# Rankings of the first sequence split by head, with their ends in PSUM and on ScalarE

## The chip, the cores and the metric

The kernel runs on one core of a Trainium2 chip. The engines are TensorE (PE in the profile: matmuls; PEld: loads of its stationary operand), VectorE (DVE), ScalarE (ACT), GpSimd (POOL) and SyncE (SP, which here only issues DMAs). The metric is the device time of one execution in microseconds (us), the median of several runs. All data are fp32.

## The reference

```python
x = x + rnn(layernorm(x))            # x: 2 sequences x 2048 tokens x 256
x = x + ffn(layernorm(x))

# ffn: attention with 8 heads of 64; 5 experts for the values and 5 for the output, 2 chosen
gl_v = (x @ Ws).reshape(b, t, h, e)              # value gates
wv   = topk_mask(gl_v, 2) * sigmoid(gl_v)
xv   = einsum('btd,edk->btek', x, Wv)            # expert values, the same for all heads
v    = einsum('bthe,btek->bhtk', wv, xv)
attn = softmax(q * scale @ k.T) @ v
mask_o = topk_mask((x @ Wd).reshape(b, t, h, e), 2)   # output gates: only a mask
out  = einsum('bthe,bthk,ekd->btd', mask_o, attn, Wo)
```

So every token has, for each of 8 heads, five value logits and five output logits. The two largest of each five are kept. Value gates are the mask times a sigmoid; output gates are the bare mask.

## The kernel before

The recurrent part runs first (to about 124 us) and leaves the first sequence's normalised tokens, transposed, in `xT_of[0]`. The rest is one long loop over **steps** W. The attention has 16 heads (8 of each sequence); each head's queries are cut into 4 blocks of 512, which makes 64 units, and a unit's keys are cut into 8 tiles. A step computes four score tiles (`scores`, L589, into a pool of three PSUM buffers), VectorE moves each to SBUF with a running minimum (`stage`, L605), and two steps later, when a unit's minimum is known (`find_low`, L616 and L618), ScalarE takes the exponentials (L621), GpSimd adds tiles up for the denominator (`add_up` and `join`, L628 to L639), and TensorE multiplies the tiles with the values (`products`, L648). So a head takes 8 steps and the second sequence begins at step 64. Engines work through their own queues in the order in which the program issues instructions.

What else belongs to a step is put in five tables by hand: `head` (issued first), `mid`, `one` (after the four scores and stages), `vec` (after the products of the step) and `two` (last). Order in one step: `head`; exponentials of the tiles two steps old; four scores with their stages; `one`; products; in odd steps `take`, ScalarE's copy of a unit's result (L659); `vec`; `two`.

The change concerns the gates:

- `experts(b, j)` multiplies two chunks of 128 tokens with the value experts and both gate matrices at once (L530). ScalarE copies the expert values to `xw` (L537) and the 80 logits of each token to the tile `gl` (L544); `xw` goes to DRAM.
- `choose` ranks the logits of 8 chunks for all heads at once. The rank array starts at 4, 3, 2, 1, 0 (ScalarE copies `base`, L183). For each difference d = 1 to 4, `pair(d)` compares expert e with expert e+d (L192, into the PSUM tile "m", of which there is one buffer), adds the result to the later expert's rank and takes it from the earlier one's (L193, L194). A rank below 1.5 is chosen. `settle` makes the sigmoid from an exponential taken at the start (L181, L182, then L199, L200), multiplies it with the mask (L201), and makes the output mask (L202). `find_low` and `gate` use the same PSUM tile "m".
- `mix` and `mix_sum` build a head's values from the gates and `xw`: for head 0 GpSimd multiplies (L571), for later heads VectorE does (L574), reading a copy of the gates that ScalarE puts in PSUM (`gate`, L558); VectorE sums (L579). A later head's expert values come back from DRAM (`fetch`, L552).
- `weigh` and `masked` (L703 to L723) apply the output gates to a unit's result, in odd steps, in the last entries of `vec`.

Before the loop come keys part 0, queries part 0 and experts 0 and 1. Step 0 then holds keys part 1, experts 2 and 3 (all in `one`), the ranking "a0" of chunks 0 to 7 and two products of gates (`vec`). Step 1 holds experts 4 to 7, queries part 1 and the ranking "a1" of chunks 8 to 15. The second sequence is ranked in ten pieces, "b0" in steps 35, 37, 39, 41, 43 and "b1" in steps 45, 47, 49, 51, 53 (`at(vec, 35 + 10 * k + 2 * j, f)`).

## Time and profile before

| what | value |
|---|---|
| three runs | 1423.73, 1426.01 (median), 1427.76 us |
| the profiled execution | 1424.15 us |
| its span, first to last instruction | 1422.3 us |
| TensorE busy | 1339.2 us (94%) |
| VectorE busy | 1135.1 us (80%) |
| GpSimd busy | 1009.3 us (71%) |
| ScalarE busy | 703.0 us (49%) |
| first product (L648) of steps 2 to 7 | 190.33, 197.53, 207.38, 215.52, 224.95, 233.09 us |
| two steps, where nothing else is going on (as 250 to 340 us) | 17.57 us |
| GpSimd adds L628, L632 | 2613, 2379 ns |
| head fetch, issue to landing | 3.9 us |

A line of the timeline or of a group has start, duration, engine, line, operation, what it writes and reads, and its shape (partitions x elements). In brackets stands how long the engine had been idle before it and what released it. A line of the waits has who waited for whom, the total in us, how many times and the longest. L numbers are lines of the kernel before, unless said otherwise.

### The profile page before, as it was taken

Reading aid. Unit: us, or ns where it says so; the run is one execution under the profiler, and the core shown is the slowest. Engines: PE = TensorE matmul, PEld = TensorE weight load, DVE = VectorE, ACT = ScalarE, POOL = GpSimd, SP = SyncE. Lnnn points to the kernel's source line nnn. Section 1 sums busy time; section 2 is a strip of 40 time slices with the busy share of each in tenths; the row PEclk is TensorE's granted clock in tenths of the full one; section 3 lists DMA queues with packets and bytes.
Section 4 is the critical chain, followed back from the end, with each engine's and each line's share of the span. In section 5 each row is a group of like instructions: output and inputs, shape, how many; then the busy total and the mean of one; then the engine's idle time right before and its main releaser. Section 6 shows DMA issues by size and latency. Waiting matters only on the chain.

```text
span 1422.3 us, 36420 instructions
## 1 busy us (share of the span) xinstructions
PE 1339.2 (94%) x15450; PEld 634.3 (45%) x15450; DVE 1135.1 (80%) x2104; ACT 703.0 (49%) x911; POOL 1009.3 (71%) x590
## 2 busy tenths in 40 slices
PE   6999689999899999989999999999999999999986
PEld 5896234444344444333344454444444444444444
DVE  6666589999877787889888787888888888888753
ACT  3434255555356556444555445555555555555451
POOL 1101168888687777778798776888888888888960
PEclk9999889999899999999999999999999999999999
DMA  6012136666666666566577555566766676767643
GB/s 193 1 67 79 63 97 155 161 146 142 130 145 146 141 132 143 120 136 132 122 162 172 123 145 142 152 134 135 150 135 149 137 151 136 150 137 151 137 106 100
DMA packets 66315, 187.00 MB, mean 131 GB/s; under 512 B 8928, under 2 KB 26464, under 8 KB 66144
## 3 DMA queue, kind: packets, MB, share of 16 engines
q0 software_dynamic: 25056, 97.53, 37.1%
q1 hardware_dynamic: 39456, 86.46, 19.2%
q8 instruction: 123, 2.02, 0.6%
q10 hardware_dynamic: 1632, 0.61, 0.2%
q14 instruction: 48, 0.39, 0.1%
HBM read 59.79 MB, written 50.33 MB: 77 GB/s over the span
## 4 chain that ended last, share of the span: by engine, by line
PE 58%; issue 15%; DVE 11%; POOL 4%; ACT 1%; DMA 1%; DVEq 0%; POOLq 0%; ACTq 0%
PE o L648 28%; PE s L589 12%; DVE p L605 7%; PE pq L505 4%; PE pk L488 4%; PE pz L825 3%; PE pv L530 3%; PE pc L667 2%; PE pc L680 1%; POOL es L632 1%; POOL es L628 1%; POOL es L638 1%; PE pl L616 1%; PE py L809 1%; DMA es<-p 1%
## 5 line engine op out<-in xcount | busy, mean ns | idle before, releaser
L605 DVE TENSOR_SCALAR_CACHE_REDUCE p<-s 128x1024 f32<-128x1024 f32 x512 | 596.4, 1221 | 116.2 <-PE s L589 114.0
L621 ACT ACTIVATE p<-p,low 128x1024 f32<-128x1024 f32 x512 | 546.1, 1140 | 54.9 <-DVE low L618 54.5
L589 PE MATMUL s<-q,k 64*32 64x512 f32 x4096 | 482.5, 603 | 13.7 <-DVE p L605 10.4
L589 PE MATMUL s<-qs,k 64*32 64x512 f32 x4096 | 482.5, 603 | 11.1 <-DVE p L605 5.8
L648 PE MATMUL o<-p,v 128*64 128x256 f32 x4096 | 472.4, 383 | 0.0
L628 POOL TENSOR_TENSOR es<-p,p 128x1024 f32<-128x1024 f32 x126 | 329.2, 2613 | 164.5 <-ACT p L621 164.5
L648 PEld LDWEIGHTS o<-p,v 128*64 128x64 f32 x4096 | 282.8, 137 | 194.6 <-ACT p L621 47.8
L632 POOL TENSOR_TENSOR es<-es,p 128x1024 f32<-128x1024 f32 x126 | 299.8, 2379 | 9.9
L659 ACT COPY os<-o 128x256 f32<-128x256 f32 x64 | 23.8, 372 | 394.7 <-PE o L648 394.7
L589 PEld LDWEIGHTS s<-qs,k 64*32 64x32 f32 x4096 | 120.7, 107 | 147.7 <-issue 75.9
L589 PEld LDWEIGHTS s<-q,k 64*32 64x32 f32 x4096 | 120.6, 107 | 147.0 <-issue 67.6
L638 POOL TENSOR_TENSOR es<-es,es 128x1024 f32<-128x1024 f32 x63 | 151.4, 2403 | 4.9 <-DMA es<-p 4.8
L634 POOL DMA_DIRECT2D es<-p x126 | 110.0, 873 | 19.1 <-POOL es L632 15.2
L574 DVE TENSOR_TENSOR pr<-xq,pw 128x1280 f32<-128x1280 f32 x60 | 89.3, 1488 | 31.1 <-ACT pw L558 31.1
L723 DVE TENSOR_TENSOR pro<-pc,mr 128x1280 f32<-128x1280 f32 (+1 forms) x65 | 95.6, 1471 | 2.2
L579 DVE TENSOR_REDUCE v<-pr 128x256 f32<-128x1280 f32 x64 | 94.9, 1485 | 2.1
L639 POOL TENSOR_TENSOR es<-es 128x512 f32<-128x512 f32 x63 | 85.5, 1358 | 4.9
L488 PE MATMUL pk<-xT,wk 128*32 128x512 f32 x512 | 62.2, 604 | 2.0 <-ACT xT L408 0.5
L505 PE MATMUL pq<-xT,wq 128*32 128x512 f32 x512 | 62.1, 603 | 1.4
L739 POOL DMA_DIRECT2D yd<-pro x48 | 56.7, 1181 | 0.8 <-DVE p L605 0.8
L571 POOL TENSOR_TENSOR pr<-xw,gates 128x1280 f32<-128x1280 f32 x4 | 11.0, 2775 | 52.2 <-DVE gates L201 52.2
L530 PE MATMUL pv<-wvg,xT 128*128 128x400 f32 x128 | 47.6, 522 | 0.0
(141 smaller groups left out, 977.2 us busy)
## 6 DMA issues: line engine op xcount, KB each, us to landing
es<-p POOLq DMA_DIRECT2D x126, 512.0 KB, 4.8
xq<-xvd SPq DMA_DIRECT2D x60, 640.0 KB, 3.9
yd<-pro POOLq DMA_DIRECT2D x48, 640.0 KB, 8.0
qs<-q SPq DMA_DIRECT2D x64, 128.0 KB, 2.3
xvd<-xw SPq DMA_DIRECT2D x8, 640.0 KB, 3.2
yd<-pro SPq DMA_DIRECT2D x8, 640.0 KB, 4.1
y<-yd SPq DMA_DIRECT2D x8, 640.0 KB, 4.8
x<-in_x SPq DMA_DIRECT2D x16, 256.0 KB, 5.1
```

What stands on the lines that cost most here:

```text
L488: nc.tensor.matmul(pk[g * R : (g + 1) * R], lhsT=wk[:, kc, d0 : d0 + R], rhs=xc[:, kc, c0 // 2 : (c0 + HC) // 2, o, :], start=kc == 0, sto ...
L505: nc.tensor.matmul(pq[g * R : (g + 1) * R, :], lhsT=wq[:, kc, d0 : d0 + R], rhs=xT_of[b][:, kc, n * QB : (n + 1) * QB], start=kc == 0, sto ...
L579: nc.vector.tensor_reduce(v_of[i][:, 4 * part : 4 * part + 4, :], pr, AX.X, ALU.add)
L589: nc.tensor.matmul(ss[g * R : (g + 1) * R, o, :], lhsT=k_of[i][half, c, g * R : (g + 1) * R], rhs=q_of[i, n][o][half, :], start=True, stop ...
L605: nc.vector.tensor_scalar(p, ss, 1.0, None, ALU.mult, ALU.min, accum_out=part_of[u][:, c : c + 1])
L621: nc.scalar.activation(ring[t], ring[t], AF.Exp, scale=-1.0, bias=low_of[t // HC])
L628: nc.gpsimd.tensor_tensor(e, ring[t], ring[t - 1], ALU.add)
L632: nc.gpsimd.tensor_tensor(e, e, ring[t], ALU.add)
L634: nc.gpsimd.dma_start(out=es_of[u, half], in_=ring[t], accum_op=ALU.add)
L638: nc.gpsimd.tensor_tensor(e, e, es_of.pop((u, 1)), ALU.add)
L648: nc.tensor.matmul(o_of[u][g * DH : (g + 1) * DH, :], lhsT=v_of[i][:, 2 * c + o, :], rhs=ring[t][:, o, g * QH : (g + 1) * QH], start=c == ...
L723: nc.vector.tensor_tensor(o_of["p", u][:, s0:s1], po[:, s0:s1].unsqueeze(2).to_broadcast([P, w, E, 2, DH]), o_of["m", u][:, s0:s1].unsquee ...
```

## The change

`choose` now takes a range of chunks and a range of heads. The first sequence is ranked in four parts: a0 (chunks 0 to 7, head 0) in step 0; a2 (chunks 0 to 7, heads 1 to 7), and after it a1 (chunks 8 to 15, head 0), in step 1; a3 (chunks 8 to 15, heads 1 to 7) in pieces in step 2 (d = 1), step 3 (d = 2 and 3) and step 4 (d = 4 and the end). The second sequence keeps its ten pieces. All logits of a sequence lie in one tile, each comparison is issued once for the value and once for the output logits, the rank array starts one lower (so that 0.5 divides), and the sigmoid is made wholly at the end, in a PSUM tile "m"; ScalarE makes the output mask with two Relu operations. keys part 1 is issued after experts 2 and 3. Head 1's mixes move from steps 3, 4, 6, 8 to 4, 5, 6, 8, and their fetches with them.

```diff
-        nc.gpsimd.memset(base[:, e : e + 1], float(E - 1 - e))
-
-    def choose(pool, scratch, b, c0, nm):
+        nc.gpsimd.memset(base[:, e : e + 1], float(E - 2 - e))
+
+    def choose(pool, scratch, b, c0, c1, h0, h1, nm):
...
+        def part(t, kind):
+            v = t.rearrange("p c (t h e) -> p c t h e", t=2, e=E)[:, c0:c1, :, h0:h1, :]
+            return v if kind is None else v[:, :, kind]
 
         def begin():
-            got[0] = pool.tile([P, G, E], F32, tag="rank", bufs=1, name=f"rank{nm}")
-            gv = gt[:, :, 0:HE]
-            nc.vector.tensor_scalar(gv, gl_of[b, c0 // HN][:, :, 0:HE], -87.0, None, ALU.max)
-            nc.scalar.activation(gv, gv, AF.Exp, scale=-1.0)
-            nc.scalar.copy(got[0], base.unsqueeze(1).to_broadcast([P, G, E]))
+            got[0] = pool.tile([P, n, 2, m, E], F32, tag="rank", bufs=1, name=f"rank{nm}")
+            for k in range(2):
+                nc.scalar.copy(
+                    got[0][:, :, k],
+                    base.unsqueeze(1).unsqueeze(1).to_broadcast([P, n, m, E]),
+                )
 
         def pair(d):
...
-            above = scratch([P, G, w], f"ge{nm}_{d}")
-            nc.vector.tensor_tensor(above, g[:, :, 0:w], g[:, :, d:], ALU.is_ge)
-            nc.vector.tensor_tensor(rank[:, :, d:], rank[:, :, d:], above, ALU.add)
-            nc.vector.tensor_tensor(rank[:, :, 0:w], rank[:, :, 0:w], above, ALU.subtract)
+            above = scratch([P, n, 2, m, w], f"ge{nm}_{d}")
+            for k in range(2):
+                nc.vector.tensor_tensor(
+                    above[:, :, k], g[:, :, k, :, 0:w], g[:, :, k, :, d:], ALU.is_ge
+                )
...
+            nc.vector.tensor_tensor(up, up, above, ALU.add)
+            nc.vector.tensor_tensor(down, down, above, ALU.subtract)
 
         def settle():
-            rank = got[0].rearrange("p (c g) e -> p c (g e)", c=8)
-            gv = gt[:, :, 0:HE]
-            nc.vector.tensor_scalar(gv, gv, 1.0, None, ALU.add)
-            nc.vector.reciprocal(gv, gv)
-            nc.vector.scalar_tensor_tensor(gv, rank[:, :, 0:HE], 1.5, gv, ALU.is_lt, ALU.mult)
-            nc.vector.tensor_scalar(gt[:, :, HE:], rank[:, :, HE:], 1.5, None, ALU.is_lt)
+            rank = got[0]
+            gv, gm = part(gates_of[b], 0), part(gates_of[b], 1)
+            sg = scratch([P, n, m, E], f"sg{nm}")
+            nc.vector.tensor_scalar(sg, part(gl_of[b], 0), -87.0, None, ALU.max)
+            nc.scalar.activation(sg, sg, AF.Exp, scale=-1.0)
+            nc.scalar.activation(gm, rank[:, :, 1], AF.Relu)
+            nc.scalar.activation(gm, gm, AF.Relu, scale=-1.0, bias=unit)
+            nc.vector.tensor_scalar(sg, sg, 1.0, None, ALU.add)
+            nc.vector.reciprocal(sg, sg)
+            nc.vector.scalar_tensor_tensor(gv, rank[:, :, 0], 0.5, sg, ALU.is_lt, ALU.mult)
...
-    for k in range(2):
+    for part in range(4):
+        k = part // 2
+        if part % 2 == 0:
+            if k:
+                for p in range(2):
+                    at(vec, 1, mix_sum, 0, p)
+                for f in choose(ap, misc, 0, 0, HN, 1, H, "a2"):
+                    at(vec, 1, f)
+            for f in choose(ap, misc, 0, k * HN, (k + 1) * HN, 0, 1, f"a{k}"):
+                at(vec, k, f)
+        at(vec, k, mix, 0, part)
...
-        else:
-            at(one, 0, keys, 0, 1)
...
-                W = max(3, W0 - 6 + 2 * part)
-                at(two if W == 3 else head, W - 1, fetch, i, part)
+                W = (4, 5, 6, 8)[part] if i == 1 else W0 - 6 + 2 * part
+                at(two if i == 1 and part in (1, 2) else head, W - 1, fetch, i, part)
...
+    at(one, 0, keys, 0, 1)
     at(one, 1, queries, 0, 1)
+    for j, f in enumerate(choose(ap, misc, 0, HN, NCH, 1, H, "a3")):
+        at(vec, 2 + (j + 1) // 2, f)
...
-        for j, f in enumerate(choose(ap, misc, 1, k * HN, f"b{k}")):
+        for j, f in enumerate(choose(ap, misc, 1, k * HN, (k + 1) * HN, 0, H, f"b{k}")):
             at(vec, 35 + 10 * k + 2 * j, f)
```

## The prediction, made before the changed kernel was run

> **What bounds the kernel now.** The page first: the 1422.3 us span has TensorE busy for 94%, and the chain that ended last gives it 58% and VectorE 11%. That is an average, so next came the timeline and waits of the stretches that hold rankings: steps 0 to 7 (134 to 236 us, step W beginning with its first score) and the second sequence's steps 35 to 53 (500 to 710 us). Waits from 134 to 204 us:
>
> ```profile
> POOL pr L571 <- DVE gates L201: 52.2, 2, 29.7
> ...
> DVE gates L181 <- ACT gl L544: 15.4, 2, 9.2
> ...
> PE s L589 <- DVE p L605: 9.7, 1, 9.7
> ...
> PE pl L616 <- DVE ranka L194: 7.3, 1, 7.3
> ```
>
> TensorE stands still twice for rankings: 9.7 us in step 1 (scores find no free buffer, since VectorE ranks until 156.99) and 7.3 us before step 2, where find_low's transpose needs the one-buffer PSUM tile that the ranking's comparisons use. The second ranking starts late, on ScalarE and VectorE:
>
> ```profile
> 174.76 0.60 ACT L515 ACTIVATE q<-pq 128x512 f32<-128x512 f32 x1 [1.00 <-PE pq L505]
> 175.25 0.46 ACT L182 ACTIVATE gates<-gates 128x320 f32<-128x320 f32 x1
> 175.61 0.71 ACT L183 COPY ranka<-base 128x640 f32<-128x640 f32 x1
> ```
>
> ```profile
> 173.79 0.33 DVE L181 TENSOR_SCALAR gates<-gl 128x320 f32<-128x320 f32 x1 [9.16 <-ACT gl L544]
> 174.04 0.69 DVE L192 TENSOR_TENSOR gea<-gl 128x512 f32<-128x512 f32 x1
> 176.36 0.69 DVE L193 TENSOR_TENSOR ranka<-ranka,gea 128x512 f32<-128x512 f32 x1 [1.63 <-ACT ranka L183]
> ...
> 182.24 2.15 DVE L200 RECIPROCAL gates<-gates 128x320 f32<-128x320 f32 x1
> ...
> 184.84 0.32 DVE L202 TENSOR_SCALAR gates<-ranka 128x320 f32<-128x320 f32 x1
> 185.07 0.28 DVE L618 TENSOR_REDUCE low<-pl 128x1 f32<-128x128 f32 x1
> ```
>
> The rank array's first fill stands in ScalarE's queue behind all expert copies and the q copy. From there to step 7's first stage, busy times of PE, PE's loads, VectorE (39.20 of 44.71 us: little slack), ScalarE, GpSimd:
>
> ```profile
> 185.07:229.78 44.71, 44.22 (x548) 18.19 (x540) 39.20 (x65) 27.99 (x32) 38.88 (x19) 0.97 0.50 124
> ```
>
> The second sequence:
>
> ```profile
> 652.13 1.51 DVE L192 TENSOR_TENSOR geb<-gl 128x256 f32<-128x256 f32 x1
> 653.67 0.46 DVE L193 TENSOR_TENSOR rankb<-rankb,geb 128x256 f32<-128x256 f32 x1
> ...
> 689.69 1.37 DVE L199 TENSOR_SCALAR gates<-gates 128x320 f32<-128x320 f32 x1
> 691.09 2.15 DVE L200 RECIPROCAL gates<-gates 128x320 f32<-128x320 f32 x1
> ```
>
> ```profile
> 650.29 3.02 POOL L628 TENSOR_TENSOR es<-p,p 128x1024 f32<-128x1024 f32 x1
> 653.38 2.50 POOL L632 TENSOR_TENSOR es<-es,p 128x1024 f32<-128x1024 f32 x1
> ```
>
> ```profile
> 691.88 0.37 ACT L659 COPY os<-o 128x256 f32<-128x256 f32 x1 [6.86 <-PE o L648]
> ```
>
> A comparison worth 0.45 us (151.50) takes 1.51: it ends just after GpSimd's L628. GpSimd's next add, 2.37 alone, is stretched to 2.50. The two exclude each other and take turns.
>
> **The change, part by part.** Prices are rows of the trace of before: VectorE pair operations 0.69, 0.57, 0.45, 0.39 us for 512, 384, 256, 128 elements and 0.17 for 20; reciprocal 2.15 for 320 and 0.19 for 4; ScalarE 0.47 for 320 and 0.17 for 20. Between them I interpolate; dependent ones add 0.03.
>
> Step 0. keys(0,1) moves behind experts 2 and 3 (5.64 us): 138.35 to 144.0, logits copied at 144.95 instead of 146.77. But the k copy now stands ahead of the rank fill: keys end 145.9, copy 146.45, two fills of 40 by 146.9 (first rank operation 148.28 before). Step 1's scores, which read these keys, wait 0.7 us more; hidden, VectorE ranks until later. Ranking a0 (8 chunks, head 0): 14 operations of 0.2 to 0.25 = 3.0, then maximum 0.2, exponential on ScalarE 0.26, add 0.2, reciprocal 0.45, select 0.2: end 151.3 (156.99 before). GpSimd's two products start there and stay hidden.
>
> Step 1. Four stages of 1.145 and "one" to 156.1, two mix sums to 159.1. TensorE: fourth score at 152.6 to 154.4, experts 4 to 7 (twice step 0's 5.64, or 12.6 as after the 9.7 us wait) to about 166.4, queries 1.9 to 168.3, q copy, then the fills of ranking a2 (7 heads, two of 280, 0.84): its first rank operation at about 169.7. So a2 cannot use the gap under the experts: only its first comparisons run there. a2: ranks 2 x 0.65, then pairs 1.8, 1.45, 1.1 = 5.65; end 0.46 + 0.49 + 0.46 + 1.95 + 0.47 = 3.8; done 179.2. a1 (chunks 8 to 15, head 0): fills wait for a2's rank buffer, 0.45 + 3.0 + 1.35 = 4.8; done T = 184.0 (182.9 to 186 with the experts' bounds). The old ranking ended 185.07, so 1.1 is gained; but find_low's transpose, at 182.03 before, now waits for a1's end, its sigmoid lying in the same PSUM tile. First product of step 2: T + 8.3 as before from the transpose: 192.3 against 190.33, **+2.0**.
>
> Steps 2 to 6. a3, another 10.9 us of VectorE work (pairs 2.1, 1.8, 1.6, 1.2, end 4.2), enters where 5.5 of 44.7 were idle; GpSimd's queue keeps its order. Step 2: pair 1 fits ahead of step 3's scores, 0. Step 3: head 1's mix (3.0) goes to step 4, pairs 2 and 3 (3.4) come, and the transpose waits for the comparison tile: +2.0 at step 4's product. Step 4: mix 3.0, pair 4 and the end. Its exponential stands in ScalarE's queue ahead of step 5's four exponentials (4.27): they move from 28 to 36 us after T. The pair meets GpSimd's join (stall 2.0). VectorE begins step 5's stages at T + 38 instead of T + 32, the fourth score waits for a buffer: +5.8. Step 5 now has mix, statistics, weigh and masked (6.1) behind its stages; masked frees a score buffer late: +2.7. From step 7 the pace is TensorE's again (17.57 per two steps), and nothing is won back. SyncE's queue: head 1's fetches go out one at a time, parts 0, 1, 2 a little later; each still follows the mix that frees its buffer by 3.9 to landing and has 7 us or more: 0; without that lead a mix would wait, 3.9 at most. The mask and weight copies of head 1 on ScalarE move with the mixes. First products of steps 2, 4, 5, 6, 7: 192, 211, 225, 237, 245 against 190, 207, 216, 225, 233. Sum **+12.4** (8 to 16).
>
> Second sequence. Each comparison becomes two, the second waiting for the first: 0.15 each, and the first loses an operation (-0.33). The price is the port: after the first half GpSimd's waiting add goes, the second half waits 2.4. Rows where two adds follow on (528.14, 548.67, 634.07, 653.38, 672.24): five, at steps 37, 39, 47, 49, 51. Steps 37 and 39 have 1.4 and 2.2 idle, leaving 1.4 and 0.8; the others 2.6 each: **+10.0** (bounds 0.6, if both halves pass together, and 13). The ends, steps 43 and 53: the exponential now stands behind the copy of o, which waits for the step's products. At 53: maximum 689.6 to 690.1, exponential 692.25 to 692.7, add 0.48, reciprocal 2.17, select 0.49: 695.9 against 694.0; at 43 595.7 against 593.4. Both lie on the chain (before: L199 to L723, then scores): **+4.1** (2 to 6). In PSUM the 320 element operations have no row of before: 0.32 to 0.49, taken at 0.48.
>
> No cost: one logits tile instead of two, the other constants, the masks on ScalarE (read first by weigh, a step or more later; two of 0.47 instead of VectorE's 0.32; without that cover the 0.6 more would fall on six endings, under 4 us). Relu has no row: at worst it reloads the function table, 1.28 once (5.55), two loads in six endings, 15 us; at best 0. I take 0: Identity, Tanh, Exp and copies ran here on a single load. The Trainium skill, "ScalarE: Activation LUTs", section "Table sets: the hidden batching unit", says that cheap functions such as relu lie in every set: by it 0 too. [...] "SBUF — State Buffer", in the consequences of its port table, says that a VectorE instruction with two SBUF inputs and a GpSimd one block each other whole and that issue order decides. It would credit the endings moved to PSUM with the stalls of L199 (0.5 and 1.05) and L181 (2.1), some 3.6 us; my sum has these, and finds more put back by halving.
>
> Sum: 12.4 + 10.0 + 4.1 = 26.5 on the profiled execution's 1424.15 (span 1422.3, 1.85 around it): **1450.6**; that execution is 1.9 under the median of three.
>
> **Rivals.**
> A, the forecast: 1450, chance 0.55.
> B, both halves of a comparison pass GpSimd together: the second sequence's 10.0 falls to 0.6, step 4's stall by 1.4: 1424.15 + 11 + 4.7 = 1440. For: consecutive operations leave gaps of 0.03. Against: L632's stretches show GpSimd already waiting. 0.2.
> C, a2 runs under the experts: VectorE idles from 159 to 169.7; T falls by 10.5, 1440 (1430 with B). Against: the queue order that L183 shows. 0.13.
> D, not slower: TensorE sets the pace and VectorE's added work is slack. For: 94% and 58%. Then steps 3 to 7 keep their 42.7, the second sequence its time: +2, 1426. It decides if steps 3 to 6 hold under 8.8 us of VectorE work; step 6 held 8.2 of 8.8 before, and 689 to 697 is VectorE's alone. 0.08. A further 0.04: faster, by some gain not seen.
>
> **How the numbers follow.** A alone spans 1443 to 1457; with B and C the range is 1435 to 1458. Under 0.3% (4.3 us) a measurement here tells nothing. Faster 0.04; same 0.06 (most of D); slower 0.90.
>
> **What would show it.** Right: a2's first rank operation near 169.7, behind two ScalarE fills; step 7's first product some 12 us later than before; second halves of comparisons near 2.7 us at steps 47, 49, 51; an idle of about 2.6 before the add of one (L215 of the changed kernel) at steps 43 and 53, released by ScalarE. Wrong: a2 under the experts, step 5's exponentials on time, or two-step periods unchanged near 650 us.

## The result and the profile after

The changed kernel takes **1447.4 us** (median of four runs, 1445.6 to 1449.23) against 1424.87 (four runs) before: a ratio of **1.0156**, 95% interval 1.0133 to 1.0179. It is slower by 22.5 us. The forecast was 1450. Executions of one kernel lie up to 0.5% apart, the longer ones with a lower mean granted clock of TensorE (the kernel before: 1422.46 us at 0.986, 1429.18 us at 0.980). The profiled execution took 1448.38 us with a span of 1446.6, that is 24.3 more than the span before.

The page of the changed kernel, busy time by engine and then the chain that ended last:

```profile
PE 1342.9 (93%) x15450; PEld 636.5 (44%) x15450; DVE 1154.6 (80%) x2156; ACT 709.0 (49%) x933; POOL 1009.7 (70%) x590
...
PE 64%; DVE 15%; issue 14%; POOL 3%; DMA 2%; ACT 2%; SPq 0%; DVEq 0%; ACTq 0%; POOLq 0%
```

TensorE, ScalarE and GpSimd do what they did before, within 6 us. VectorE works 19.5 us more (1154.6 against 1135.1), and its share of the chain went from 11% to 15% (TensorE's from 58% to 64%). That already says in which queue to look, but not where.

To find the places, take one event that both kernels have in every odd step, ScalarE's copy of a unit's result `o`, and subtract its start in the profile before from its start in another profile. This **delay** rises where time is lost and stays level where nothing happens. What VectorE does at the end of an odd step shows at the copy of the next odd step. In us:

| profile | first stage | 3 | 5 | 7 | 9 | 35 | 43 | 45 | 53 | 55 | 127 |
|---|---|---|---|---|---|---|---|---|---|---|---|
| kernel before, a second profile | 0.7 | 0.8 | 0.9 | 0.8 | 0.8 | 0.9 | 0.9 | 0.9 | 0.9 | 0.9 | 0.7 |
| changed kernel | 1.4 | 2.5 | 11.1 | 12.4 | 12.8 | 12.1 | 13.2 | 14.7 | 21.8 | 23.3 | 24.3 |

So the 24.3 us consist of 1.4 before the first stage, where no code was changed; 11.4 up to step 9, the first sequence's rankings; 1.1 for the comparisons of steps 35 to 41 and 7.1 for those of steps 45 to 51; 1.5 and 1.6 for the endings at steps 43 and 53; and about 0.3 for the rest. The second row of the table shows what such a difference is worth: two profiles of the same program are 0.7 to 0.9 apart. These are sums by place and not yet by cause: in steps 4 and 5 a part is TensorE's granted clock ("Steps 3 to 7" below).

Steps 0 and 1, waits from 134 to 204 us of the changed kernel (who waited for whom, the total, how many times, the longest):

```profile
PE pl L630 <- DVE gates L217: 15.8, 1, 15.8
ACT sga L212 <- DVE sga L211: 12.9, 3, 6.3
DVE ranka L204 <- ACT ranka L184: 11.3, 2, 9.9
PE s L603 <- DVE p L619: 2.9, 1, 2.9
```

The wait of the scores for VectorE fell from 9.7 to 2.9 us: head 0 alone is ranked sooner. But two waits have come in its place. VectorE waits 9.9 us for the fill of a2's rank array, and the transpose of `find_low` (L630) waits 15.8 us instead of 7.3 for a ranking, now for its last instruction. ScalarE's timeline there, and VectorE's:

```profile
169.44 0.60 ACT L530 ACTIVATE q<-pq 128x512 f32<-128x512 f32 x1 [1.00 <-PE pq L520]
169.93 0.74 ACT L184 COPY ranka<-base 128x280 f32<-128x280 f32 x2
```

```profile
159.94 0.82 DVE L197 TENSOR_TENSOR gea<-gl 128x224 f32<-128x224 f32 x2
170.71 0.62 DVE L204 TENSOR_TENSOR ranka<-ranka,gea 128x448 f32<-128x448 f32 x1 [9.94 <-ACT ranka L184]
...
185.73 0.29 DVE L632 TENSOR_REDUCE low<-pl 128x1 f32<-128x128 f32 x1 [0.56 <-PE pl L630]
...
222.15 1.22 DVE L619 TENSOR_SCALAR_CACHE_REDUCE p<-s 128x1024 f32<-128x1024 f32 x1
```

The two fills are at the end of ScalarE's queue, behind the expert copies and the q copy, just as the fill was before; a2's comparisons are ready at 160.8 and the first rank operation starts at 170.71. Step 5's first stage (L619) starts at 222.15.

The second sequence, step 47 and the ending at step 53, on VectorE, then GpSimd at step 47 and ScalarE at step 53:

```profile
647.47 3.86 DVE L197 TENSOR_TENSOR geb<-gl 128x192 f32<-128x192 f32 x2
...
714.38 0.50 DVE L215 TENSOR_SCALAR sgb<-sgb 128x320 f32<-128x320 f32 x1 [2.44 <-ACT sgb L212]
```

```profile
645.63 3.04 POOL L642 TENSOR_TENSOR es<-p,p 128x1024 f32<-128x1024 f32 x1
648.75 2.35 POOL L646 TENSOR_TENSOR es<-es,p 128x1024 f32<-128x1024 f32 x1
```

```profile
713.65 0.37 ACT L673 COPY os<-o 128x256 f32<-128x256 f32 x1 [6.87 <-PE o L662]
713.92 0.43 ACT L212 ACTIVATE sgb<-sgb 128x320 f32<-128x320 f32 x1
```

The two halves of one comparison take 3.86 us together. They begin while GpSimd's L642 is running and end at 651.33, just after L646 ends at 651.10: the second half has waited for a whole further add. In step 53 the exponential (L212) starts behind the copy of `o`, which waits for the products, and VectorE is idle 2.44 us.

### The profile page after: what moved, and what is told of

Its sections match the earlier page's. It is cut to its first block, busy times and chain, and to the rows that moved or that the text cites. A ratio compares the mean times of both kernels' runs of the same rounds, so it can differ in the third digit from the quotient of the medians.

```text
span 1446.6 us, 36493 instructions
## 1 busy us (share of the span) xinstructions
PE 1342.9 (93%) x15450; PEld 636.5 (44%) x15450; DVE 1154.6 (80%) x2156; ACT 709.0 (49%) x933; POOL 1009.7 (70%) x590
## 3 DMA queue, kind: packets, MB, share of 16 engines
q8 instruction: 123, 2.02, 0.6%
## 4 chain that ended last, share of the span: by engine, by line
PE 64%; DVE 15%; issue 14%; POOL 3%; DMA 2%; ACT 2%; SPq 0%; DVEq 0%; ACTq 0%; POOLq 0%
PE o L662 28%; PE s L603 12%; DVE p L619 7%; PE pq L520 4%; PE pk L503 4%; PE pv L545 3%; PE pz L839 3%; PE pc L681 2%; PE phb L315 2%; PE px L298 1%; PE pc L694 1%; PE pha L315 1%; DVE geb L197 1%; PE pl L630 1%; POOL es L652 1%
## 5 line engine op out<-in xcount | busy, mean ns | idle before, releaser
L619 DVE TENSOR_SCALAR_CACHE_REDUCE p<-s 128x1024 f32<-128x1024 f32 x512 | 596.8, 1221 | 114.8 <-PE s L603 111.5
L642 POOL TENSOR_TENSOR es<-p,p 128x1024 f32<-128x1024 f32 x126 | 329.4, 2614 | 186.8 <-ACT p L635 186.8
L646 POOL TENSOR_TENSOR es<-es,p 128x1024 f32<-128x1024 f32 x126 | 299.5, 2377 | 9.9
L673 ACT COPY os<-o 128x256 f32<-128x256 f32 x64 | 23.9, 373 | 393.9 <-PE o L662 393.9
L630 PE MATMUL pl<-ident,one 128*128 128x128 f32 x64 | 20.5, 320 | 36.1 <-DVE gates L217 24.0
```

Source lines behind the costliest of these rows:

```text
L619: nc.vector.tensor_scalar(p, ss, 1.0, None, ALU.mult, ALU.min, accum_out=part_of[u][:, c : c + 1])
L642: nc.gpsimd.tensor_tensor(e, ring[t], ring[t - 1], ALU.add)
L646: nc.gpsimd.tensor_tensor(e, e, ring[t], ALU.add)
```

## The experiments

Unless said otherwise an edit is made to the changed kernel. Kernels were compared with the kernel before in the same session, where it took 1424.6 to 1426.0 us (medians). The delays of all of them, in the columns of the table above. Each row is one profiled execution, which can lie up to 2.6 us from the median of its kernel: v1's took 1416.15 us (median 1418.70), v2's 1421.61 (1419.21), e9's 1448.80 (1446.72).

| profile | first stage | 3 | 5 | 7 | 9 | 35 | 43 | 45 | 53 | 55 | 127 |
|---|---|---|---|---|---|---|---|---|---|---|---|
| changed kernel | 1.4 | 2.5 | 11.1 | 12.4 | 12.8 | 12.1 | 13.2 | 14.7 | 21.8 | 23.3 | 24.3 |
| e1_one_compare | 1.7 | 2.7 | 11.3 | 12.6 | 13.0 | 12.3 | 12.1 | 13.6 | 13.4 | 16.0 | 17.5 |
| e2_early_exp | 1.6 | 2.7 | 11.2 | 12.6 | 12.9 | 12.3 | 13.7 | 12.3 | 20.6 | 18.9 | 18.4 |
| e3_fill_early | 1.9 | -3.9 | 4.8 | 5.9 | 6.3 | 6.1 | 7.1 | 8.6 | 15.4 | 16.9 | 17.8 |
| e4_first_as_before | 1.6 | 5.8 | 5.9 | 5.8 | 5.9 | 5.2 | 6.2 | 7.8 | 14.5 | 16.1 | 15.3 |
| e5_a3_early_exp | 2.0 | 2.6 | 11.2 | 12.1 | 12.4 | 13.9 | 14.9 | 16.1 | 23.2 | 24.7 | 25.6 |
| e6_first_sbuf_end | 1.8 | 2.7 | 2.7 | 2.7 | 2.7 | 2.6 | 3.7 | 5.2 | 11.9 | 13.5 | 14.7 |
| e8_a3_relu_later | 1.1 | 2.6 | 13.4 | 14.3 | 14.6 | 14.6 | 15.7 | 17.2 | 23.9 | 25.4 | 26.7 |
| e9_a3_less_vector | 2.9 | 2.2 | 6.9 | 9.4 | 9.4 | 8.5 | 9.6 | 12.4 | 19.5 | 21.9 | 23.0 |
| v1_split_filled | 2.3 | -5.4 | -5.4 | -5.4 | -5.4 | -6.2 | -6.1 | -7.7 | -6.9 | -8.0 | -7.9 |
| v2_add_on_scalar | 1.9 | -3.6 | -3.6 | -3.6 | -3.6 | -4.0 | -3.3 | -5.0 | -4.3 | -4.5 | -4.3 |

### Is it the halving of the comparisons?

```
             above = scratch([P, n, 2, m, w], f"ge{nm}_{d}")
-            for k in range(2):
+            if m == H:
+                gf = gl_of[b][:, c0:c1, :].rearrange("p c (g e) -> p (c g) e", e=E)
                 nc.vector.tensor_tensor(
-                    above[:, :, k], g[:, :, k, :, 0:w], g[:, :, k, :, d:], ALU.is_ge
+                    above.rearrange("p c t h e -> p (c t h) e"), gf[:, :, 0:w], gf[:, :, d:], ALU.is_ge
                 )
+            else:
+                for k in range(2):
...
```

> The changed kernel, with each comparison of the second sequence's rankings issued as one operation over all groups, as before the change; nothing else. Theory (the second half of a comparison lets GpSimd's waiting add go first and then waits for it): the comparisons of steps 35 to 51, now 2.8 to 3.9 us, fall to 0.5 to 2.9 with one add in each at most; the delay against the kernel before that builds up from step 35 to step 51 (from 12.1 to 21.8 us in the traces, less 1.5 at step 43) goes, so 7 to 9 us less than the changed kernel's 1447.4: about 1439. Rival 1 (the halves cost only their own fixed time, 0.15 us each): 1 us less, 1446. Rival 2 (the delay there comes from the pace of TensorE, not from comparisons): no change.

Measured: 1440.68 us (1439.77 to 1441.87), ratio 1.0100 (1.0074 to 1.0126), 6.7 us under the changed kernel. Up to step 35 the delays are those of the changed kernel. From 35 to 43 the delay falls by 0.3 instead of rising by 1.1, and from 45 to 53 by 0.2 instead of rising by 7.1. VectorE's comparisons at steps 47, 49 and 51 of this kernel:

```profile
646.59 1.22 DVE L198 TENSOR_TENSOR geb<-gl 128x384 f32<-128x384 f32 x1
...
665.52 1.52 DVE L198 TENSOR_TENSOR geb<-gl 128x256 f32<-128x256 f32 x1
...
684.41 1.45 DVE L198 TENSOR_TENSOR geb<-gl 128x128 f32<-128x128 f32 x1
```

In the changed kernel these three were 3.86, 3.18 and 3.74 as pairs. The single comparison also waits for GpSimd, but once: it gets its turn when the running add ends. So the cost of halving isn't the fixed cost of a second instruction but a second place in the line. Of the 8.2 us, 1.0 came back later: the ending at step 53 cost 2.6 here. Behind it the granted clock is 0.50 for 6.8 us (708.0 to 714.8), in the changed kernel for 3.4 us (718.2 to 721.6).

### Is it the exponential's place in ScalarE's queue?

```
+        early = m == H
+
         def begin():
+            if early:
+                gv = part(gates_of[b], 0)
+                nc.vector.tensor_scalar(gv, part(gl_of[b], 0), -87.0, None, ALU.max)
+                nc.scalar.activation(gv, gv, AF.Exp, scale=-1.0)
...
         def settle():
...
-            sg = scratch([P, n, m, E], f"sg{nm}")
-            nc.vector.tensor_scalar(sg, part(gl_of[b], 0), -87.0, None, ALU.max)
-            nc.scalar.activation(sg, sg, AF.Exp, scale=-1.0)
+            if early:
+                sg = gv
+            else:
...
```

> The changed kernel, with the second sequence's exponentials taken at the start of each ranking (maximum on VectorE and exponential on ScalarE, into the gates in SBUF) as before the change, not in the last piece. Theory (at steps 43 and 53 VectorE waits 2.4 us for an exponential that stands behind the copy of o): the waits go, but add and maximum meet GpSimd's adds again, 0.1 to 1 us each; delays of 1.5 and 1.6 us go, 0 to 0.7 us come back at steps 35 and 45: 2 to 3 us less, 1444.5 to 1445.5. Rival (the wait is hidden, scores are not ready earlier): no change.

Measured: 1442.95 us (1441.27 to 1444.54), ratio 1.0119 (1.0091 to 1.0146), 4.45 us less than the changed kernel and more than I had forecast (2 to 3). The delay falls by 1.4 over the ending at step 43 and by 1.7 over that at step 53; in the changed kernel it rises by 1.5 and 1.6. The addition of 1 at these two endings, on VectorE:

```profile
603.33 1.02 DVE L224 TENSOR_SCALAR gates<-gates 128x320 f32<-128x320 f32 x1
...
710.29 0.75 DVE L224 TENSOR_SCALAR gates<-gates 128x320 f32<-128x320 f32 x1
```

No idle time stands in front of it. It still loses some time to GpSimd (with 280 elements it took 0.30 where it lost none, below), but far less than the 2.44 that it waited for ScalarE. Against the kernel before such an ending lacks the output mask, which ScalarE now makes; that is 0.32 of the gain. The addition stood at 0.83 there in step 43 and at 1.37 in step 53. And the mix that follows waits 0.46 and 0.47 us for its weights here, against 1.83 and 1.19 in the kernel before. Those longer waits go with the granted clock: behind the two endings it is 0.50 for 3.4 us in the kernel before (from 597.0 and 696.0 us) and in the changed kernel (from 609.0 and 718.2), and 1.00 throughout here (600 to 625 and 700 to 725).

### Does a2 really miss its gap through the fill?

```
         def pair(d):
-            if d == 1:
+            if d == 1 and 0 not in got:
                 begin()
...
-        return [lambda d=d: pair(d) for d in range(1, E)] + [settle]
+        return [lambda d=d: pair(d) for d in range(1, E)] + [settle, begin]
...
+    a2 = choose(ap, misc, 0, 0, HN, 1, H, "a2")
...
         at(vec, k, mix, 0, part)
+        if part == 1:
+            at(vec, 0, a2[-1])
```

> The changed kernel, with the two fills of a2's rank array issued on ScalarE at the end of step 0, ahead of the copies of experts 4 to 7; nothing else. Theory (a2 can't run under the experts because its fill stands behind their copies and the q copy): a2's first rank operation moves from 170.7 to about 161 us; its end still needs an exponential that stands behind the q copy (until 170), so a2 ends near 173.3 instead of 180.3 and a1 near 178 instead of 185.2. 7 us less, 1440. Rival (TensorE, not the ranking, sets the start of step 2): the product of step 2 stays, no change.

Measured: 1441.97 us (1439.95 to 1443.5), ratio 1.0106 (1.0079 to 1.0133), 5.4 us under the changed kernel. The delay at step 3 is 6.4 lower, and it stays so up to step 55. VectorE's timeline around a2's start, and at the beginning of step 2:

```profile
160.49 0.82 DVE L197 TENSOR_TENSOR gea<-gl 128x224 f32<-128x224 f32 x2
161.41 0.62 DVE L204 TENSOR_TENSOR ranka<-ranka,gea 128x448 f32<-128x448 f32 x1
...
170.91 0.46 DVE L215 TENSOR_SCALAR sga<-sga 128x280 f32<-128x280 f32 x1 [3.22 <-ACT sga L212]
...
179.25 0.29 DVE L632 TENSOR_REDUCE low<-pl 128x1 f32<-128x128 f32 x1 [0.57 <-PE pl L630]
```

The 9.94 us of idle time are gone, and 3.22 come back at a2's ending, whose exponential again stands behind the expert copies on ScalarE: 9.9 - 3.2 = 6.7, close to what arrived. Two copies of 0.37 us each, ready long before they are wanted but issued too late, cost over 6 us.

### What does the split of the rankings by head cost after step 2?

The first sequence is ranked whole in steps 0 and 1 again, with the new operations:

```
-    for part in range(4):
-        k = part // 2
-        if part % 2 == 0:
+    for k in range(2):
+        if k:
+            for part in range(2):
+                at(vec, k, mix_sum, 0, part)
+        for f in choose(ap, misc, 0, k * HN, (k + 1) * HN, 0, H, f"a{k}"):
+            at(vec, k, f)
...
-                W = (4, 5, 6, 8)[part] if i == 1 else W0 - 6 + 2 * part
+                W = max(3, W0 - 6 + 2 * part)
...
-    for j, f in enumerate(choose(ap, misc, 0, HN, NCH, 1, H, "a3")):
-        at(vec, 2 + (j + 1) // 2, f)
```

> The changed kernel, with the first sequence's rankings in two whole parts in steps 0 and 1 as before the change (head 1's mixes at steps 3, 4, 6, 8 again), but with the new operations: halved comparisons, and ends in PSUM. Theory (head by head ranking costs VectorE 11 us more that nothing hides): the 11.4 us of delay that build up from step 0 to step 9 go, less about 3.5 us, since the transpose of find_low now waits for a1's end in the PSUM tile: 8 us less, 1439.5. Rival (the new operations are what costs, not the split): the delay at step 9 stays, 1446 or more.

Measured: 1442.64 us (1439.47 to 1444.47), ratio 1.0112 (1.0082 to 1.0142). The delay is 5.8 at step 3 and 5.9 at step 9: flat, where the changed kernel loses 10.3 between the same steps. So that staircase belongs to a3 and to the moved mixes, which this run takes back together. What is left, 5.8 at step 3, 4.2 more than at the first stage, must come from the new ending. The waits from 134 to 204 us:

```profile
PE pl L630 <- DVE gates L217: 11.9, 1, 11.9
```

The transpose that waited 7.3 us for the comparisons now waits for the ending, since the sigmoid occupies the only buffer of the PSUM tile "m". To test this, the exponential and the sigmoid of the first sequence went to SBUF as well, as in the second experiment:

```
+        early = m == H and b == 0
+
         def begin():
+            if early:
+                gv = part(gates_of[b], 0)
...
-            sg = scratch([P, n, m, E], f"sg{nm}")
+            if early:
+                sg = gv
+            else:
...
```

> As the run with the first sequence ranked whole in steps 0 and 1, with one thing more: the first sequence's exponentials are taken at the start of each ranking and the sigmoid is made in SBUF, as before the change, so that its end no longer holds the PSUM tile. In the run without it the first copy of o came 5.85 us later than in the kernel before, of which about 1.6 were there at the first stage. Theory (find_low's transpose waits for the end of the ranking because its sigmoid lies in the tile): the transpose comes 3 to 4 us sooner against the end of a1, and the 5.85 fall to 2 to 2.5, the time by 3 to 4 us, to about 1439. Rival (halved comparisons are the cost there): under 1 us.

Measured: 1437.9 us (1436.3 to 1439.1), ratio 1.0082 (1.0057 to 1.0107). The delay falls to 2.7 at all steps from 3 to 9, of which 1.8 were there at the first stage. The same wait, and the minimum that follows the transpose, on VectorE:

```profile
PEld pl L639 <- DVE ranka L211: 8.9, 1, 8.9
```

```profile
187.19 0.49 DVE L226 SCALAR_TENSOR_TENSOR gates<-ranka,gates 128x320 f32<-128x320 f32 x1
187.60 0.28 DVE L641 TENSOR_REDUCE low<-pl 128x1 f32<-128x128 f32 x1
```

It waits for the last rank operation (L211) again, and the minimum follows the select without idle time. The new ending costs 3.2 us in all. That isn't the tile's share alone, since this run also takes the maximum and the exponential out of the ending: from the last rank operation to the end of the select VectorE needs 2.9 us here and 4.2 in e4. So 1.3 can be VectorE's longer ending, and about 1.9 is left for the wait for the tile. The two were not taken apart.

### Steps 3 to 7: ScalarE's queue or VectorE's work?

The prediction put the 5.8 us at step 5 down to a3's exponential, which holds step 5's exponentials back on ScalarE. The rival is that VectorE simply ranks too long. First a3's maximum and exponential alone went to its start in step 2:

```
+        early = nm == "a3"
+
         def begin():
+            if early:
+                gv = part(gates_of[b], 0)
+                nc.vector.tensor_scalar(gv, part(gl_of[b], 0), -87.0, None, ALU.max)
+                nc.scalar.activation(gv, gv, AF.Exp, scale=-1.0)
...
```

> The changed kernel, with a3's exponential taken at its start in step 2 (maximum on VectorE, exponential on ScalarE into the gates in SBUF) instead of at its end in step 4, so that in step 4 ScalarE's queue no longer holds it ahead of step 5's four exponentials. It settles which of two things makes step 5 late. If it is VectorE's own work (forecast: 3.3 us of ending stay, 1 us of waiting for the exponential goes): the first copy of o after step 5, 11.1 us behind the kernel before, comes 1 to 1.5 us sooner and the time falls as much, to about 1446. If it is ScalarE's queue (the exponentials of step 5 came 8 us later than before): they start at about 214.5 instead of 220.1, and 4 to 6 us go, 1442.

Measured: 1449.02 us (1446.09 to 1452.36), ratio 1.0163 (1.0129 to 1.0196): nothing gained, a miss for both sizes that I had given. From step 4's minimum to step 5's first stage VectorE now takes 14.8 us instead of 16.0, as the first theory has it. But 0.9 us had been lost before that: the exponential moved to step 2 holds back step 3's exponentials on ScalarE (196.47 instead of 194.05), GpSimd's second add comes later (201.20 instead of 199.50) and meets step 3's comparisons, which take 1.59 us instead of 0.71. It doesn't decide between the two, since ScalarE's Relu was still waiting for the rank in front of the exponentials:

```profile
219.37 0.44 ACT L222 ACTIVATE gates<-ranka 128x280 f32<-128x280 f32 x1 [4.50 <-DVE ranka L211]
...
220.28 4.25 ACT L644 ACTIVATE p<-p,low 128x1024 f32<-128x1024 f32 x4
```

So the two Relus were also moved, to the end of step 5:

```
...
+            if not early:
+                masks()
...
+        def masks():
+            gm = part(gates_of[b], 1)
+            nc.scalar.activation(gm, got[0][:, :, 1], AF.Relu)
+            nc.scalar.activation(gm, gm, AF.Relu, scale=-1.0, bias=unit)
+
-        return [lambda d=d: pair(d) for d in range(1, E)] + [settle]
+        return [lambda d=d: pair(d) for d in range(1, E)] + [settle] + [masks] * early
```

> The changed kernel with a3's maximum and exponential at its start in step 2, and its two Relus behind step 5's exponentials, at the end of step 5: ScalarE's queue holds nothing of a3's ending between the copy of the mix weights at 213.8 and step 5's exponentials, which start at 220.12 in the changed kernel. Both theories have them start near 214. Theory 'ScalarE's queue', as the prediction had it: they held the step back, so the copies of o at steps 5, 7 and 9 come 4 to 6 us earlier than in the changed kernel (delays of 5 to 7, 6 to 8 and 7 to 9 us against 11.1, 12.4 and 12.8), median about 1442 to 1444. Theory 'VectorE's work': the score buffers wait for VectorE, which ranks until about 222 whatever ScalarE does; step 5's first stage stays at 221.3 to 222.3, the delays within 1 us of 11.1, 12.4 and 12.8, median 1446 to 1449.

Measured: 1452.69 us (1451.47 to 1455.47), ratio 1.0196 (1.0178 to 1.0213). ScalarE's timeline and VectorE's in step 4:

```profile
213.18 4.27 ACT L649 ACTIVATE p<-p,low 128x1024 f32<-128x1024 f32 x4
```

```profile
216.22 2.07 DVE L203 TENSOR_TENSOR gea<-gl 128x56 f32<-128x56 f32 x2
...
218.86 2.65 DVE L224 TENSOR_SCALAR gates<-gates 128x280 f32<-128x280 f32 x1
...
223.99 1.21 DVE L633 TENSOR_SCALAR_CACHE_REDUCE p<-s 128x1024 f32<-128x1024 f32 x1
```

The exponentials start 6.9 us earlier than in the changed kernel (220.12 there), and step 5 doesn't come earlier but 1.8 us later. VectorE works without a pause from step 4's mix on, and step 5's first stage follows its select. Three things made it later. Step 3's comparisons take 1.57 us instead of 0.71, as in the run before. Step 4's comparisons take 2.07 instead of 0.76: they end with GpSimd's join of step 4 (216.87 to 218.16), which is no earlier than in the changed kernel (215.95), so the early exponentials aren't the reason, and the next run has the same 2.05 without them. The addition of 1 takes 2.65 (an operation of this kind takes 0.30 in v1_split_filled, below): it ends with GpSimd's first add of step 5 (218.69 to 221.33), and that add is early because its exponentials are. Finally VectorE's work was cut, with ScalarE's queue as in the changed kernel:

```
-            nc.vector.tensor_scalar(sg, sg, 1.0, None, ALU.add)
-            nc.vector.reciprocal(sg, sg)
+            if nm != "a3":
+                nc.vector.tensor_scalar(sg, sg, 1.0, None, ALU.add)
+                nc.vector.reciprocal(sg, sg)
```

> The changed kernel without the addition of 1 and the reciprocal of a3's sigmoid (0.46 and 1.92 us of VectorE work in step 4; the value gates of seven heads and half of the first sequence are then not sigmoids). ScalarE's queue is as in the changed kernel, its step 5 exponentials near 220.1. Theory 'VectorE's work': step 5's first stage comes at 219.7 to 219.9 instead of 222.15, the delays at steps 5, 7 and 9 fall by 2.0 to 2.5 us (8.6 to 9.1 at step 5), median 1445. Theory 'ScalarE's queue': nothing is gained, the delays at 5, 7 and 9 stay within 0.7 us of 11.1, 12.4 and 12.8.

Measured: step 5's first stage starts at 219.09 instead of 222.15, and the delay from step 3 to step 9 grows by 7.2 us instead of 10.3. These 3.1 us, for 2.4 us of VectorE work less, are more than either theory had. Step 5's exponentials are 0.6 us earlier:

```profile
215.02 2.05 DVE L197 TENSOR_TENSOR gea<-gl 128x56 f32<-128x56 f32 x2
...
219.09 1.22 DVE L620 TENSOR_SCALAR_CACHE_REDUCE p<-s 128x1024 f32<-128x1024 f32 x1
```

```profile
219.51 4.25 ACT L636 ACTIVATE p<-p,low 128x1024 f32<-128x1024 f32 x4
```

From the start of step 4's mix to step 5's first stage VectorE takes 7.0 us instead of 8.17: the 2.4 that were left out, less 1.3 that the comparisons lose to GpSimd's join. This stretch is VectorE's alone. The rest of the gain is TensorE's. The windows of its scores in step 4 and of the time behind step 5's first stage (the last numbers are the granted clock, DMA share and GB/s), in the changed kernel and then in this one:

```profile
206.20:209.60 3.40, 3.40 (x40) 1.07 (x32) 1.43 (x3) 3.17 (x4) 0.89 (x1) 0.50 0.04 7
223.30:226.60 3.30, 3.17 (x28) 0.81 (x30) 3.30 (x7) 1.14 (x3) 3.22 (x2) 0.50 0.00 0
```

```profile
206.20:209.60 3.40, 3.35 (x68) 0.89 (x56) 2.63 (x5) 3.40 (x4) 1.21 (x1) 1.00 0.02 5
223.30:226.60 3.30, 3.30 (x35) 1.85 (x39) 3.23 (x5) 0.90 (x3) 3.20 (x2) 1.00 0.15 19
```

In the changed kernel TensorE runs at half clock in both, here and in the kernel before at the full clock. From step 4's minimum to its mix the changed kernel takes 7.87 us, this one 6.30; from step 5's first stage to the copy of `o` 8.15 and 6.96 (the kernel before 6.97). So of the 3.9 us by which this run is faster between the copies of steps 3 and 5, 1.2 are the edit's and 2.8 the clock's. Ahead of step 4's scores TensorE had been idle for 2.02 us in both; why the clock fell in one and not in the other was not found.

VectorE's work decides, not the place of the exponentials: here they start 0.4 us after step 5's first stage, and the copy of `o` comes as long after that stage as in the kernel before, where they start 4.2 us ahead of it. What TensorE's clock adds to that is a cost that neither theory had.

The time was 1446.72 us (1444.32 to 1448.8), ratio 1.0145 (1.0128 to 1.0161), only 0.7 under the changed kernel: the profile has 1.5 us more ahead of the first stage, and the endings at steps 43 and 53 cost 2.9 and 2.5 instead of 1.5 and 1.6. In all three places the granted clock is 0.50 for 6.8 us (24.4 to 31.2, 604.7 to 611.5 and 713.9 to 720.7) and in the changed kernel for 3.4 (25.3 to 28.7, 609.0 to 612.4 and 718.2 to 721.6).

### The parts that help, without those that cost

v1 keeps head 0's early ranking in step 0 (a0), ranks the other seven heads of chunks 0 to 7 in the gap under the experts (a2, its fill and exponential issued at the end of step 0), ranks chunks 8 to 15 whole (a1, no a3), leaves head 1's mixes in steps 3, 4, 6 and 8, and makes whole rankings with single comparisons and an early exponential in SBUF:

```
+        early = m == H or nm == "a2"
...
-            for f in choose(ap, misc, 0, k * HN, (k + 1) * HN, 0, 1, f"a{k}"):
+            for f in choose(ap, misc, 0, k * HN, (k + 1) * HN, 0, (1, H)[k], f"a{k}")[:-1]:
                 at(vec, k, f)
         at(vec, k, mix, 0, part)
+        if part == 1:
+            at(vec, 0, a2[-1])
...
-                W = (4, 5, 6, 8)[part] if i == 1 else W0 - 6 + 2 * part
+                W = max(3, W0 - 6 + 2 * part)
...
-    for j, f in enumerate(choose(ap, misc, 0, HN, NCH, 1, H, "a3")):
-        at(vec, 2 + (j + 1) // 2, f)
```

> Put together from what the runs showed: a0 for head 0 alone in step 0; a2 with its fill and exponential on ScalarE at the end of step 0, so that it runs under experts 4 to 7; a1 for all heads in step 1, no a3 (head 1's mixes at steps 3, 4, 6, 8); whole rankings (a1 and the second sequence) with single comparisons and the sigmoid in SBUF. Theory: a2's first rank operation at 161, its end near 169.5; a1's ranks from 170.7 to 176.5, the transpose of find_low at 176.5 against 182.0 in the kernel before, step 2's product 5.5 us sooner (less 1.5 that the changed kernels start later); second sequence as before. 4 to 6 us under the kernel before: about 1420. Rival (step 2 is bound by queries part 1 and its copies, at 170): it gains no more than 2 us, 1424 or more.

Measured: **1418.7 us** (1416.15 to 1420.36), ratio **0.9955** (0.9935 to 0.9974): 6.5 us faster than the kernel before in the same session (1425.17), and 28.7 faster than the changed kernel. VectorE's timeline of step 1 up to step 2's minimum:

```profile
161.09 0.82 DVE L209 TENSOR_TENSOR gea<-gl 128x224 f32<-128x224 f32 x2
162.01 0.62 DVE L216 TENSOR_TENSOR ranka<-ranka,gea 128x448 f32<-128x448 f32 x1
...
167.73 0.30 DVE L230 TENSOR_SCALAR gates<-gates 128x280 f32<-128x280 f32 x1
...
171.93 0.69 DVE L216 TENSOR_TENSOR ranka<-ranka,gea 128x512 f32<-128x512 f32 x1 [0.63 <-ACT ranka L190]
...
180.41 0.28 DVE L647 TENSOR_REDUCE low<-pl 128x1 f32<-128x128 f32 x1
```

a2 now runs from 161 to 170, under the experts, and step 2's minimum comes at 180.41 (before: 185.07), although the first stage was 2.3 us later. Of the 7.9 us that this profile gains, 5.4 stand at step 3. Another 1.7 come from step 35 on, where little but the output mask differs from the kernel before; the kernel before has three stretches of 3.4 us at half clock there (597, 617 and 696 us), this profile has one (610.6).

v2 also moves the addition of 1 to ScalarE, behind the exponential, since it lost time to GpSimd in v1:

```
                 nc.scalar.activation(gv, gv, AF.Exp, scale=-1.0)
+                nc.scalar.activation(gv, gv, AF.Identity, bias=unit)
...
-            nc.vector.tensor_scalar(sg, sg, 1.0, None, ALU.add)
+            if not early:
+                nc.vector.tensor_scalar(sg, sg, 1.0, None, ALU.add)
```

> The run with the split and filled rankings, and the sigmoid's add of one made on ScalarE right behind the exponential instead of on VectorE. Theory (VectorE alone sets steps 43 and 53, where that add took 0.8 and 1.4 us in the kernel before, with a wait for GpSimd): 1.5 to 2.5 us less than without it, about 1418. Rival (the wait for GpSimd moves to the next operation with two SBUF inputs): 0.5 us less.

Measured: 1419.21 us (1417.65 to 1421.61), ratio 0.9948 (0.9926 to 0.9969): no difference from v1 that these runs show. VectorE at the ending of step 43 in v1, and then in v2:

```profile
583.53 0.85 DVE L230 TENSOR_SCALAR gates<-gates 128x320 f32<-128x320 f32 x1
...
586.60 0.49 DVE L232 SCALAR_TENSOR_TENSOR gates<-rankb,gates 128x320 f32<-128x320 f32 x1
```

```profile
588.51 1.26 DVE L234 SCALAR_TENSOR_TENSOR gates<-rankb,gates 128x320 f32<-128x320 f32 x1
```

The stall didn't go, it moved to the next instruction that GpSimd excludes, the select (1.26 instead of 0.49). The larger part of the difference between the two profiles lies elsewhere, in the first sequence (1.8 us at step 3): a1's first rank operation waits 2.80 us for its fill here and 0.63 in v1. That was not followed up.

### Is the late first stage the program's or the run's?

The kernel before, unchanged, once more:

> The kernel before, unchanged, in a second profile. In the first profile its first stage of the first score tile starts at 135.91 us; in the profiles of the changed kernel and of all its variants it starts 1.4 to 2.3 us later, though nothing ahead of it was edited. If that lateness belongs to the run, this profile too has its first stage at 137 to 138.5 us, and its span is 1 to 2 us longer than 1422.3. If it belongs to the program (its instructions lie elsewhere), the first stage is within 0.4 us of 135.9 again.

Measured: first stage at 136.63, 0.7 later than in the first profile and earlier than in any variant (137.0 to 138.8), so neither of the two cases as I had put them. The profile shows what differs. TensorE at 24 to 30 us, in the kernel before (second profile) and in the changed kernel:

```profile
26.05 0.66 PE L271 MATMUL tpa<-ident,xn 128*128 128x128 f32 x4 [2.50 <-ACT xn L248]
26.55 1.89 PE L283 MATMUL px<-xnT,wi 128*128 128x256 f32 x8
```

```profile
25.06 0.93 PE L286 MATMUL tpa<-ident,xn 128*128 128x128 f32 x4 [3.57 <-ACT xn L263]
25.78 3.35 PE L298 MATMUL px<-xnT,wi 128*128 128x256 f32 x8
```

The same eight matmuls take 1.89 us in one and 3.35 in the other. The windows from 26.0 to 28.5 us (busy time of PE, its loads, VectorE, ScalarE, GpSimd, then the granted clock), before and after:

```profile
26.00:28.50 2.50, 2.45 (x15) 2.20 (x16) 2.36 (x9) 1.71 (x5) 1.67 (x4) 1.00 0.04 11
```

```profile
26.00:28.50 2.50, 2.50 (x7) 1.96 (x7) 1.70 (x5) 0.69 (x2) 0.71 (x2) 0.50 0.00 0
```

The granted clock is 0.50 after an idle time of 3.57 us and 1.00 after one of 2.50. At this place it is so in all profiles: 2.60 and 2.50 in the two of the kernel before, with the clock at 1.00; 3.56 to 3.58 in the changed kernel and all ten variants, with the clock at 0.50 for 3.4 us (6.8 in e9). It is no rule for other places: at step 4 the changed kernel drops to half clock after 2.02 us of idle time. Why TensorE runs dry earlier at 25 us, with the same instructions in the same order, is open: the group of eight `px` matmuls at 17 us took 3.35 and 3.46 us in the kernel before and 1.9 to 2.0 in the others (the granted clock is given as 1.00 for all), so that these were done sooner and then waited longer for the next tokens.

## Why the prediction came out right, and where it didn't

- **The direction and the size.** The sum was 26.5 us; 24.3 were lost between the two profiles, 22.5 between the medians. Its three terms were 12.4, 10.0 and 4.1; measured 11.4, 8.2 and 3.1. All three are a little too large, and 1.4 of the 24.3 lie in front of the first stage, in a place that the prediction didn't speak of. That the total comes so near is partly luck: the granted clock, which no term of the sum contains, took the place of stalls that did not fall due.
- **Steps 0 and 1: right.** a2's first rank operation was put at 169.7 and came at 170.71, with the first stage 1.4 late; T was put at 184.0 and came at 185.17. Rival C, a2 under the experts, (put at 1440) is what e3 makes of the kernel by issuing the fill earlier: 1441.97, but with T 6.5 us sooner and not the 10.5 that C put, since the exponential is still late.
- **Step 2's wait for the PSUM tile: right in kind.** The term was +2.0 for the kernel as changed. Its first product came at 192.78, 2.45 later than before, of which 1.4 were there at the first stage, so 1.1 is the step's own. e4 and e6, with the ending of a whole ranking in it, measure 3.2 for the ending in PSUM as a whole.
- **Steps 3 to 7: the size right, the reason in part wrong.** "VectorE begins step 5's stages at T + 38" came at T + 37. In these 37 are 1.6 us that TensorE's half clock cost in step 4, and 1.2 more follow behind the stage (e9); the prediction had nothing for the clock. And its chain of causes went through "its exponential stands in ScalarE's queue ahead of step 5's four exponentials". With those four 6.9 us earlier (e8) nothing is gained; with 2.4 us less on VectorE (e9) step 5's first stage comes 1.2 sooner after the mix, which is those 2.4 less a stall of 1.3. The place in the queue was a symptom. "The pair meets GpSimd's join (stall 2.0)" did not happen in the changed kernel (0.76), but does in e8 and e9 (2.07, 2.05), where the two engines are shifted against each other: whether such a stall falls due is a matter of a microsecond.
- **The halved comparisons: the mechanism right, the sum 1.8 too large.** All eight second halves took 2.37 to 2.48 us, where five rows were named and some 2.7 put for three of them; where VectorE has idle time behind them they cost little. Step 45, where nothing was put, gave 0.6 back, and steps 47, 49 and 51 cost 3.4, 1.6 and 2.6 instead of 2.6 each. Rival B, both halves pass together, is refuted by the pairs of 2.8 to 3.9 us and by e1.
- **The endings: right in kind, 1.0 too large.** The idle of "about 2.6" before the addition was 2.44 at both endings. e2 removes it, and the ending without it is 1.4 to 1.7 shorter than before: 0.32 for the mask on ScalarE, 0.6 for the shorter addition at step 53 alone, and 1.4 and 0.7 of shorter waiting behind the endings, where the kernel before runs at half clock and e2 does not.
- **What was costed at nothing.** Relu brought no second load of the function table: the profile after has one load of 1283 ns, as before. The Trainium skill's statement on this ("ScalarE: Activation LUTs", section "Table sets: the hidden batching unit") agrees with it.
- **Rival D, not slower,** fell with step 5: VectorE had no room left for a3.

## What to carry to other kernels

An operation that is moved takes its place in a queue on every engine it touches: look for the small helper (a fill, an exponential) on the other engine, what stands ahead of it there, and issue it as soon as its inputs exist. Where two engines exclude each other, count instructions and not only their durations, since each further one can wait for a whole instruction of the other; and expect a stall that is removed from one instruction to turn up at the next. A symptom that stands right in front of a delay, as the late exponentials did here, is only a cause if moving it moves the delay. And lay the granted clocks of two profiles side by side before a difference between them is given to an edit: in e9 2.8 of 3.9 us were the clock's.

## What the runs showed of the hardware that was not expected

- At 25 us an idle time of TensorE of 3.56 to 3.58 us was followed by half the granted clock for 3.4 us (6.8 in e9), one of 2.5 to 2.6 us was not; the first stage came 0.4 to 2.2 us later than in the later of the two profiles of the kernel before. The Trainium skill ("TensorE: Matmul & The Clock Gate", section "What's actually happening") names some 3.4 us of idleness as what takes the clock down. At 25 us these numbers lie on either side of it; at step 4 they don't agree with it: 2.02 us of idle time were followed by half clock in the changed kernel (206.2 to 209.6), while 2.02 in e9 and 2.88 in e8 were not. The length of an idle time alone doesn't decide it in these traces.
- VectorE's addition of a constant, with one input and one output in SBUF, is also held up by GpSimd: 0.30 us for 280 elements in v1 where GpSimd was idle, 2.65 for the same in e8. With its input and output in PSUM it took 0.46 and 0.50 for 280 and 320 elements in the changed kernel (219.34 and 714.38), the second while a GpSimd add was running (712.35 to 714.70). The prediction set such stalls of the kernel before (L199, L181) beside the skill's sentence on two SBUF inputs; these instructions have one.
- Exponentials made 6.9 us earlier (e8) did not help: they let GpSimd's add start earlier as well, and it met VectorE's addition of 1 (2.65 us). The median was 5.3 us above that of the changed kernel. In the profiles, whose spans are 4.3 apart, 1.8 stand at step 5's first stage, 2.4 at step 127 and the rest behind it; that rest was not followed up.
